# Layer 3 of a four-layer image kernel: a sum of squares on TensorE, two one-operand sums on ScalarE

## The chip, the cores and the metric

The kernel runs on one core of a Trainium2 chip. The metric is the device time of one execution in microseconds (us): the median of three runs is 34541.69 us, from 34539.79 to 34548.45.

## The reference, cut to what matters

Four layers follow one another on an image of 256x256 positions with 128 channels, all in fp32: an attention layer, a state-space layer, a Fourier layer, and a gated complex recurrence with 16 steps. Each adds to its input, after a group normalisation. Only the fourth (called layer 3) is touched. Its core, for every position and 64 complex channels, is:

```python
forget_gate = jax.nn.sigmoid(x_ri @ Wf + bf + 2.0)
input_gate = jax.nn.sigmoid(x_ri @ Wi + bi)
delta = jax.nn.softplus(x_ri @ Wd + bd) * 0.1
...
Ar, Ai = (A_ri[..., :c], A_ri[..., c:])
mag = jnp.sqrt(Ar ** 2 + Ai ** 2 + 1e-08)
scale = 0.95 * jax.nn.sigmoid(mag) / (mag + 1e-08)
Ar = Ar * scale
Ai = Ai * scale
...
def step(h_state, _):
    h_r, h_i = h_state
    Ah_r = Ar * h_r - Ai * h_i
    Ah_i = Ar * h_i + Ai * h_r
    return ((fg_r * Ah_r + inp_r, fg_i * Ah_i + inp_i), None)
```

A_ri and B_ri are the two-dimensional spectra of small 7x7 kernels. The kernel replaces the 16 steps by a closed form: the step is a 2x2 matrix, whose 16th power and the sum of whose powers follow from its determinant d and half trace t by repeated squaring.

## The kernel before, in words

The program runs one layer after the other. Layer 3 (layer3, L1358) works through 64 blocks of 1024 positions. A block is held as 8 tiles of 128 positions; `full` is [128, 8, 2, 64] (real and imaginary parts, 1024 elements in each partition) and `half` is [128, 8, 64] (512 elements). Five generators hold the work of a block:

- spectra(b) (L1416) loads x and the column spectra, evaluates the row spectra with eight matmuls (tile sps, L1428; two of them share one of two PSUM banks), copies them to sp by ScalarE (L1432), squares them (amp, L1435), adds the two squares (sq, L1437, VectorE), takes the magnitude as exp(0.5 ln) (mag, L1440 and L1441), adds 1e-8 (more, L1444, VectorE), and calls inverse (L1406): a first reciprocal by ln and exp on ScalarE (m_r, L1409 and L1410) and a correction of two VectorE operations (m_i, L1412 and L1413).
- gates(b) (L1448) takes the sigmoid of mag (sg, L1451), and for each of the 8 tiles makes two matmuls into one of three PSUM banks (gp, L1456 with the data, L1457 with the bias) and two ScalarE reads of it (fi, a sigmoid, L1458; dx, a copy, L1459).
- inputs(b) (L1463) makes the scale, the softplus (tail, L1474 to L1476, then L1489 and L1491), the squared size (sizes, L1479, which reads sq) and the input v.
- steps(b) (L1495) makes d (two products, L1507), t and their squares (L1511, ScalarE), x = 1 - t (L1541, VectorE), den (L1543), its inverse (d_r and d_i), and the two combinations that end in mv (L1567) and v (L1568).
- finish(b) (L1571) sums minus mv, minus v and the transposed x in PSUM (rp, L1579 to L1582), copies that out by ScalarE (o, L1585) and stores it.

The main loop (L1599) goes block by block. In its first half it alternates gates(b) with the first four parts of steps(b-1), and runs finish(b-2); in its second half it alternates the rest of steps(b-1), inputs(b) and spectra(b+1). ScalarE has two sets of tables to switch between in every block: one for ln and exp (loaded at L1606) and one for the sigmoid (loaded at L1451).

Two things set the order in which instructions stand in the queues. ScalarE keeps the order in which the program is written (L1595 asks for a written-out schedule of that engine alone). For the other engines a planner chooses the order when the program is built, from its own costs; the order is fixed from then on, and each engine takes its instructions in that order. From the third block on, every block has the same order on VectorE, and nearly every one on TensorE.

[...] Layer 3 uses seven: three for gp, two for sps, two for rp.

Of the kernel before, what the change touches and what calls it, by code (L numbers as in the profile page):

```python
# [10 lines left out]
F32 = mybir.dt.float32  # L11
AF = mybir.ActivationFunctionType
ALU = mybir.AluOpType
AX = mybir.AxisListType
PSUM = bass.MemoryType.PSUM
# [1342 lines left out]
def layer3(c, x3, out, ab):  # L1358
# [4 lines left out]
    tc, nc, t = c.tc, c.nc, c.t  # L1363
# [3 lines left out]
    full, half = [P, NT, 2, 64], [P, NT, 64]  # L1367
    with ExitStack() as a:
# [5 lines left out]
        wk = a.enter_context(tc.tile_pool(name="l3_wk", bufs=2))  # L1374
        tmp = a.enter_context(tc.tile_pool(name="l3_tmp", bufs=1))
        ps_g = a.enter_context(tc.tile_pool(name="l3_pg", bufs=3, space=PSUM))
        ps_s = a.enter_context(tc.tile_pool(name="l3_ps", bufs=2, space=PSUM))
        ps_r = a.enter_context(tc.tile_pool(name="l3_pr", bufs=2, space=PSUM))

        wall = one.tile([P, 4, P], F32, name="l3_wall")  # L1380

# [14 lines left out]
        tiny = one.tile([P, 1], F32, name="l3_tiny")  # L1396
# [3 lines left out]
        def swapped(m):  # L1400
            return m[:, :, ::-1]

        def twice(m):
            return m[:, :, None].to_broadcast(full)

        def inverse(x, scale, name):  # L1406

            first = tmp.tile(half, F32, name=f"{name}_r")
            nc.scalar.activation(first, x, AF.Ln, scale=scale)  # L1409
            nc.scalar.activation(first, first, AF.Exp, scale=-1.0)  # L1410
            inv = wk.tile(half, F32, name=f"{name}_i")
            nc.vector.scalar_tensor_tensor(inv, x, scale, first, ALU.mult, ALU.mult)  # L1412
            nc.vector.scalar_tensor_tensor(inv, inv, 2.0, first, ALU.subtract, ALU.mult)  # L1413
            return inv

        def spectra(b):  # L1416

            k = blocks[b] = {}
            k["x"] = io.tile([P, BL], F32, name="l3_x")
            nc.sync.dma_start(k["x"], x3[:, bass.ts(b, BL)])  # L1420
            tu = io.tile([14, 4, 256], F32, name="l3_tu", bufs=2)
            nc.sync.dma_start(tu, spec[bass.ts(b, 4)].rearrange("u r f -> r u f"))

            sp = k["sp"] = wk.tile([P, NT, 4, 64], F32, name="l3_sp")
            for i in range(NT):
                if i % 2 == 0:
                    sps = ps_s.tile([P, 2, 256], F32, name="l3_sps")
                nc.tensor.matmul(  # L1428
                    sps[:, i % 2], phase[:, bass.ts(i % 2, P)], tu[:, i // 2], start=True, stop=True
                )  # L1430
                if i % 2 == 1:
                    nc.scalar.copy(sp[:, i - 1 : i + 1].rearrange("p t k c -> p t (k c)"), sps)  # L1432
            yield
            amp = tmp.tile(full, F32, name="l3_amp")
            nc.scalar.activation(amp, sp[:, :, 0:2], AF.Square)  # L1435
            sq = k["sq"] = wk.tile(half, F32, name="l3_sq")
            nc.vector.tensor_tensor(sq, amp[:, :, 0], amp[:, :, 1], ALU.add)  # L1437
            yield
            mag = k["mag"] = wk.tile(half, F32, name="l3_mag")
            nc.scalar.activation(mag, sq, AF.Ln, bias=tiny)  # L1440
            nc.scalar.activation(mag, mag, AF.Exp, scale=0.5)  # L1441
            yield
            more = tmp.tile(half, F32, name="l3_more")
            nc.vector.tensor_scalar(more, mag, 1e-8, None, ALU.add)  # L1444
            k["inv"] = inverse(more, 1.0, "l3_m")
            yield

# [47 lines left out]
        def steps(b):  # L1495


            k = blocks[b]
            f, aa, v = k["fi"][:, :, 0:2], k["aa"], k["v"]
            have = {}  # L1500

            def new(name):
                return have.get(name) or tmp.tile(half, F32, name=f"l3_{name}")

            def mul(name, x, y):
                have[name] = new(name)
                nc.vector.tensor_tensor(have[name], x, y, ALU.mult)  # L1507

            def square(name, x):
                have[name] = new(name)  # L1510
                nc.scalar.activation(have[name], x, AF.Square)  # L1511

            def stt(name, x, s, y, op0, op1):
                have[name] = new(name)
                nc.vector.scalar_tensor_tensor(have[name], x, s, y, op0, op1)

            w = have

            mv = k["mv"] = wk.tile(full, F32, name="l3_mv")
            mu = tmp.tile(full, F32, name="l3_mu")  # L1520
            mul("d", f[:, :, 0], f[:, :, 1])
            mul("d", w["d"], k["size"])
            square("d2", w["d"])
            square("d4", w["d2"])
            have["f"] = new("f")
            nc.vector.tensor_tensor(w["f"], f[:, :, 0], f[:, :, 1], ALU.add)
            mul("t", aa[:, :, 0], w["f"])
            square("t2", w["t"])
            square("d8", w["d4"])
            yield  # L1530
            nc.vector.tensor_tensor(mv, v, twice(aa[:, :, 0]), ALU.mult)
            stt("t2", w["d"], -2.0, w["t2"], ALU.mult, ALU.add)
            square("t4", w["t2"])
            yield
            nc.vector.tensor_tensor(mu, swapped(v), twice(aa[:, :, 1]), ALU.mult)
            stt("t4", w["d2"], -2.0, w["t4"], ALU.mult, ALU.add)
            square("t8", w["t4"])
            yield
            stt("m", w["t"], 2.0, w["t2"], ALU.mult, ALU.mult)
            have["x"] = new("x")  # L1540
            nc.vector.tensor_scalar(w["x"], w["t"], -1.0, 1.0, ALU.mult, ALU.add)  # L1541
            have["den"] = new("den")
            nc.vector.tensor_tensor(w["den"], w["x"], w["d"], ALU.add)  # L1543
            stt("t8", w["d4"], -2.0, w["t8"], ALU.mult, ALU.add)
            square("tt8", w["t8"])
            yield
            mul("m", w["m"], w["t4"])
            w["inv"] = inverse(w["den"], 2.0, "l3_d")
            mul("m", w["m"], w["t8"])
            yield  # L1550
            stt("e", w["m"], 0.5, w["t"], ALU.mult, ALU.mult)
            stt("e", w["d8"], 2.0, w["e"], ALU.mult, ALU.add)
            have["ee"] = new("ee")
            nc.vector.tensor_tensor(w["ee"], w["e"], w["tt8"], ALU.subtract)
            nc.vector.tensor_tensor(mv[:, :, 0], mv[:, :, 0], mu[:, :, 0], ALU.subtract)
            yield
            stt("a", w["ee"], 2.0, w["m"], ALU.add, ALU.subtract)
            mul("md", w["m"], w["d"])
            stt("b", w["ee"], 2.0, w["x"], ALU.add, ALU.mult)
            nc.vector.tensor_tensor(mv[:, :, 1], mv[:, :, 1], mu[:, :, 1], ALU.add)  # L1560
            yield
            nc.vector.tensor_tensor(w["b"], w["b"], w["md"], ALU.add)
            nc.vector.tensor_tensor(mv, mv, f, ALU.mult)
            mul("a", w["a"], w["inv"])
            mul("b", w["b"], w["inv"])
            yield
            nc.vector.tensor_tensor(mv, mv, twice(w["a"]), ALU.mult)  # L1567
            nc.vector.tensor_tensor(v, v, twice(w["b"]), ALU.mult)  # L1568
            yield
# [25 lines left out]
        a.enter_context(tc.manual_schedule(engines={mybir.EngineType.Activation}))  # L1595
        tc.keep_in_program_order(nc.scalar.preload_act_table_set(EXP_LN))
        run(spectra(0))
        going = iter(())
        for b in range(NB + 2):  # L1599
            turns = gates(b) if b < NB else iter(())  # L1600
            for i in range(4):
                next(turns, None)
                next(going, None)
                if i == 1 and b >= 2:
                    run(finish(b - 2))
            tc.keep_in_program_order(nc.scalar.preload_act_table_set(EXP_LN))  # L1606
            run(
                going,
                *([inputs(b)] if b < NB else []),
                *([spectra(b + 1)] if b + 1 < NB else []),  # L1610
            )
            going = steps(b) if b < NB else iter(())
# [107 lines left out]
```

## Time and profile before

| | |
|---|---|
| median of three runs | 34541.69 us |
| the profiled execution, its own time | 34537.54 us |
| its span, first to last instruction | 34535.8 us |
| layer 3 with the preparation of its kernels' spectra | from about 32380 us to the end of the span, 2156 us |
| VectorE busy in these 2156 us | 2044.7 us |
| TensorE busy (matmul) in them | 1791.8 us |
| ScalarE busy in them | 1505.0 us |
| GpSimd busy in them | 0 us |
| mean granted TensorE clock in them | 0.81 |

The profile comes from one execution. PE is TensorE's matmuls and PEld its weight loads, DVE is VectorE, ACT is ScalarE, POOL is GpSimd; L1437 is line 1437 of the kernel. Tile names are cut, so that l_sq stands for l3_sq. One fp32 matmul leaves two records, and the ends of matmuls are modelled, so that starts are the better measure of their rate. An arrow (<-) behind a group or an instruction names what released it after an idle time; such releasers are inferred. A busy share is not a bound by itself: what counts is which wait ends last.

### The profile page before, as it was taken

The numbers are of one execution on the slowest core, as the hardware profiler recorded it, in microseconds if no ns is written. First come the engines' busy times: TensorE is split into PE (matmuls) and PEld (weight loads), VectorE is DVE, ScalarE is ACT, GpSimd is POOL, SyncE is SP. The second block draws the span as 40 slices with busy tenths as digits, with TensorE's granted clock in tenths as the row PEclk, the third lists the DMA queues.
The fourth block names the chain that finished last, engine by engine and source line by source line (L and its number), as shares of the span: only waits on it lengthen the run. The fifth ranks groups of instructions, "written<-read, shape, count | busy, mean of one in ns | idle before, by whom it ended". The sixth has DMA issues, their size and how long they took to land. (4 is left out here: it accounts for less than half of the span.)

```text
span 34535.8 us, 255681 instructions
## 1 busy us (share of the span) xinstructions
PE 29222.5 (85%) x72564; PEld 12231.8 (35%) x72564; DVE 31354.0 (91%) x24089; ACT 22500.8 (65%) x46445; POOL 26717.0 (77%) x6484
## 2 busy tenths in 40 slices
PE   7999888888888888888888888888888888899888
PEld 2554333333333333333333333333333333334444
DVE  5668899999999999999999999999999999863699
ACT  3665577777777777777777777777777777532476
POOL 2441199999999999999999999999999999620000
PEclk8999999999999999999999999999999999999888
DMA  3113655555555555555555555555555555674111
GB/s 136 45 45 99 155 190 190 191 191 191 189 191 191 190 190 192 191 190 191 195 201 200 202 201 199 202 204 200 201 202 200 201 202 202 213 236 147 66 34 33
DMA packets 2367335, 5947.80 MB, mean 172 GB/s; under 512 B 637447, under 2 KB 1639704, under 8 KB 1792086
## 3 DMA queue, kind: packets, MB, share of 16 engines
q1 hardware_dynamic: 2230742, 5864.31, 47.6%
q10 hardware_dynamic: 135168, 67.13, 0.6%
q8 instruction: 572, 9.37, 0.1%
q14 instruction: 853, 6.99, 0.1%
HBM read 5238.41 MB, written 692.58 MB: 172 GB/s over the span
## 5 line engine op out<-in xcount | busy, mean ns | idle before, releaser
L769 DVE TENSOR_TENSOR_SCAN l1b_h<-l1b_da,l1b_state,l1b_db 128x1024 f32<-128x1024 f32 x8192 | 18793.1, 2336 | 596.1 <-ACT l1b_db L758 583.8
L784 POOL TENSOR_TENSOR l1b_hc<-l1b_h,l1b_cc 128x2048 f32<-128x2048 f32 x4096 | 18446.0, 4528 | 329.2 <-DVE l1b_h L769 328.4
L803 PE MATMUL l1b_y<-l1b_hc,ident 128*128 128x512 f32 x32768 | 16052.8, 639 | 1117.9 <-POOL l1b_hc L784 1117.8
L754 ACT ACTIVATE l1b_da<-l1b_dl,l_A 128x512 f32<-128x512 f32 (+1 forms) x16384 | 11297.5, 690 | 3156.7 <-DVE l1b_h L769 2848.5
L803 PEld LDWEIGHTS l1b_y<-l1b_hc,ident 128*128 128x128 f32 x32768 | 6524.5, 205 | 10687.1 <-issue 8157.6
L736 POOL TENSOR_TENSOR l1b_db<-l1b_bb,l1b_dus 128x2048 f32<-128x2048 f32 x1536 | 6966.8, 4536 | 1245.2 <-DMA l1b_bb<-l1b_bc 1245.2
L736 DVE TENSOR_TENSOR l1b_db<-l1b_bb,l1b_du 128x2048 f32<-128x2048 f32 x2048 | 4658.4, 2275 | 35.2
L758 ACT ACTIVATE l1b_db<-l1b_state,l1b_db,l1b_af 128x1 f32<-128x1 f32 x8192 | 3045.1, 372 | 0.0
L675 PE MATMUL l1b_mm<-l1b_xd,l_dtw 41*128 41x512 f32 x2048 | 1374.6, 756 | 1714.1 <-ACT l1b_dus L725 1708.3
L701 PE MATMUL l1b_mm<-l1b_tail,ident 128*128 128x512 f32 x2048 | 1292.2, 717 | 1388.4 <-ACT l1b_tail L695 1388.4
L780 ACT COPY l1b_state<-l1b_h 128x4 f32<-128x4 f32 x4095 | 789.7, 193 | 2433.5 <-DVE l1b_h L769 2433.4
L326 POOL TENSOR_TENSOR l0b_e<-l0b_e,l0b_den 128x1024 f32<-128x1024 f32 x512 | 969.0, 1893 | 1403.0 <-DVE l0b_den L325 784.3
L701 PE MATMUL l1b_mm<-l1b_relu,ident 128*128 128x512 f32 x2048 | 1307.4, 727 | 0.0
L675 PEld LDWEIGHTS l1b_mm<-l1b_xd,l_dtw 41*128 41x128 f32 x2048 | 338.0, 206 | 2528.5 <-ACT l1b_dus L725 2131.4
L725 ACT COPY l1b_dus<-l1b_mm 128x512 f32<-128x512 f32 x512 | 299.6, 585 | 1388.2 <-DVE l1b_db L736 1387.7
L736 DVE TENSOR_TENSOR l1b_db<-l1b_bb,l1b_mm 128x2048 f32<-128x2048 f32 x512 | 1171.5, 2288 | 18.2 <-ACT l1b_dus L725 0.7
L302 DVE CUSTOM_DVE_ANT_0 l0b_e<-l0b_sc,l0b_bias 128x256 f32<-128x256 f32 x2048 | 745.5, 420 | 419.0 <-PE l0b_sc L291 415.7
L701 PEld LDWEIGHTS l1b_mm<-l1b_tail,ident 128*128 128x128 f32 x2048 | 377.1, 207 | 2059.0 <-ACT l1b_tail L695 1814.6
L493 DVE SCALAR_TENSOR_TENSOR l1a_mm<-l1a_xi,l1a_each,l1a_mm 128x512 f32<-128x512 f32 x1408 | 1046.1, 755 | 59.1 <-issue 13.0
L643 PE MATMUL l1b_du<-l1b_xc,l_xproj 128*40 128x512 f32 x2048 | 981.5, 602 | 62.4 <-DMA l_xproj<-in_l_xproj 58.8
L317 ACT ACTIVATE l0b_e<-l0b_e,l0b_top 128x256 f32<-128x256 f32 x2048 | 1012.2, 498 | 1.9 <-DVE l0b_top L302 1.9
L709 ACT COPY l1b_dl<-l1b_mm 128x512 f32<-128x512 f32 x1024 | 587.5, 574 | 524.5 <-DVE l1b_du L717 517.0
(256 smaller groups left out, 28744.8 us busy)
## 6 DMA issues: line engine op xcount, KB each, us to landing
l1b_bb<-l1b_bc SPq DMA_DIRECT2D x2048, 1024.0 KB
l1b_cc<-l1b_bc SPq DMA_DIRECT2D x2048, 1024.0 KB
l1b_xc<-l_xc SPq DMA_DIRECT2D x128, 1024.0 KB
l_y<-l1b_yo SPq DMA_DIRECT2D x128, 1024.0 KB
l1b_xc<-l_xct SPq DMA_DIRECT2D x128, 1024.0 KB
l_y<-l1b_yo SPq DMA_DIRECT2D x256, 512.0 KB
l_xc<-l1a_o SPq DMA_DIRECT2D x64, 1024.0 KB
l_xct<-l1a_ot SPq DMA_DIRECT2D x16, 4096.0 KB
```

Of the source, the lines that this page charges most:

```text
L317: nc.scalar.activation(e[:, i], e[:, i], AF.Exp, scale=-1.0, bias=top[:, i : i + 1], accum_out=den[:, i : i + 1],)
L326: nc.gpsimd.tensor_tensor(e, e, den[:, :, None].to_broadcast([P, 4, S]), ALU.mult)
L493: nc.vector.scalar_tensor_tensor(mm, xis[i][:, r + dy : r + dy + 2, dx : dx + S], each[:, dh, tap : tap + 1], mm, ALU.mult, ALU.add,)
L643: nc.tensor.matmul(du1[:40], w["xproj"][:, dh, k, :], blocks[ch][0][:, dh, cols(ch)], start=dh == 0, stop=dh == 1,)
L675: nc.tensor.matmul(mm, w["dt"][:, chunks[ch][0], dh * P : dh * P + P], xds[ch % 3][0:41], start=True, stop=True,)
L701: nc.tensor.matmul(mm, c.ident, part, start=i == 0, stop=i == 1)
L736: eng.tensor_tensor(db, bbs[g // 2], du[:, None, :].to_broadcast([P, G, CH]), ALU.mult)
L754: nc.scalar.activation(da[:, o + lo : o + hi], dl[:, lo:hi], AF.Exp, scale=w["A"][:, k, dh, n : n + 1])
L758: nc.scalar.activation(first, states[k][:, dh, two : two + 1], AF.Identity, scale=af[:, two : two + 1], bias=first,)
L769: nc.vector.tensor_tensor_scan(h_, a_, d_, states[k][:, dh, one : one + 1], ALU.mult, ALU.add)
L784: nc.gpsimd.tensor_tensor(hc, hs[g], ccs[g // 2], ALU.mult)
L803: nc.tensor.matmul(ys[j % 2], c.ident, hc[:, i], start=False, stop=j // 2 * G + i == 15)
```

## The change

Three operations leave VectorE. The sum of the two squares, sq, becomes two accumulating matmuls of the identity with the two halves of amp, into a PSUM bank that no other tile uses (a new pool with one buffer, the eighth bank); mag and sizes then read sq from PSUM. The addition of 1e-8, more, and the negation x = 1 - t become activations of ScalarE with the function Identity, with a pointer operand as the bias. Nothing else is edited. In the changed program lines after the new pool are moved down by one, those after the sum by two.

```diff
@@ -1376,6 +1376,7 @@
         ps_s = a.enter_context(tc.tile_pool(name="l3_ps", bufs=2, space=PSUM))
         ps_r = a.enter_context(tc.tile_pool(name="l3_pr", bufs=2, space=PSUM))
+        ps_q = a.enter_context(tc.tile_pool(name="l3_pq", bufs=1, space=PSUM))
@@ -1433,15 +1434,16 @@
             amp = tmp.tile(full, F32, name="l3_amp")
             nc.scalar.activation(amp, sp[:, :, 0:2], AF.Square)
-            sq = k["sq"] = wk.tile(half, F32, name="l3_sq")
-            nc.vector.tensor_tensor(sq, amp[:, :, 0], amp[:, :, 1], ALU.add)
+            sq = k["sq"] = ps_q.tile(half, F32, name="l3_sq")
+            for i in range(2):
+                nc.tensor.matmul(sq, c.ident, amp[:, :, i], start=i == 0, stop=i == 1)
             yield
             mag = k["mag"] = wk.tile(half, F32, name="l3_mag")
             nc.scalar.activation(mag, sq, AF.Ln, bias=tiny)
             nc.scalar.activation(mag, mag, AF.Exp, scale=0.5)
             yield
             more = tmp.tile(half, F32, name="l3_more")
-            nc.vector.tensor_scalar(more, mag, 1e-8, None, ALU.add)
+            nc.scalar.activation(more, mag, AF.Identity, bias=tiny)
             k["inv"] = inverse(more, 1.0, "l3_m")
@@ -1538,7 +1540,7 @@
             have["x"] = new("x")
-            nc.vector.tensor_scalar(w["x"], w["t"], -1.0, 1.0, ALU.mult, ALU.add)
+            nc.scalar.activation(w["x"], w["t"], AF.Identity, scale=-1.0, bias=c.ones[:, 0:1])
             have["den"] = new("den")
             nc.vector.tensor_tensor(w["den"], w["x"], w["d"], ALU.add)
```

## The prediction

> **What bounds the kernel now.** I went from the page's slices to the groups by line, the sums over stretches, the waits, and last the instructions of one block in order of time. The changed lines run only after 32380 us, in layer 3 (64 blocks); the first fence gives that stage and then three consecutive blocks, each from one load of the exp/log table (L1606) to the next. Columns: stretch, length, busy time (x instructions) of PE, PEld, DVE, ACT, POOL, granted clock, DMA share, GB/s.
>
> ```profile
> 32380.00:34536.00 2156.00, 1791.78 (x4608) 942.76 (x4608) 2044.69 (x2816) 1505.02 (x2754) 0.00 (x0) 0.81 0.11 33
> ...
> 32998.87:33032.47 33.60, 28.49 (x74) 15.17 (x73) 32.45 (x45) 23.43 (x43) 0.00 (x0) 0.80 0.11 34
> 33032.47:33066.07 33.60, 28.50 (x74) 14.95 (x73) 32.45 (x46) 23.52 (x44) 0.00 (x0) 0.80 0.11 33
> 33066.07:33097.97 31.90, 26.80 (x74) 14.24 (x73) 30.74 (x44) 23.43 (x44) 0.00 (x0) 0.84 0.12 35
> ```
>
> A block takes 33.03 us on average; VectorE (DVE) is busy but for 1.15 us. So layer 3 looks VectorE-bound, and the three removed operations are its own. But the block is also a ring through all engines. Two of the removed groups (count, busy us, mean ns, idle before), and the waits of the stage (who waited for whom: us in total, times, longest):
>
> ```profile
> L1541 DVE TENSOR_SCALAR l_x<-l_t 128x512 f32<-128x512 f32 x61 | 25.8, 423 | 0.0
> L1444 DVE TENSOR_SCALAR l_more<-l_mag 128x512 f32<-128x512 f32 x61 | 25.6, 420 | 0.0
> ```
> ```profile
> ACT l_d L1511 <- DVE l_d L1507: 194.3, 60, 3.2
> ...
> DVE l_sq L1437 <- ACT l_amp L1435: 67.4, 60, 1.3
> ACT l_mag L1440 <- DVE l_sq L1437: 46.8, 61, 1.3
> ```
>
> ScalarE (ACT) issues in written order. It has only 3.24 us of slack per block, at d (L1511). One block in order of time (start, length), ACT, then PE, then DVE:
>
> ```profile
> 33010.04 1.06 ACT L1435 ACTIVATE l_amp<-l_sp 128x1024 f32<-128x1024 f32 x1
> 33011.86 0.72 ACT L1440 ACTIVATE l_mag<-l_sq,l_tiny 128x512 f32<-128x512 f32 x1 [0.76 <-DVE l_sq L1437]
> 33012.61 0.63 ACT L1441 ACTIVATE l_mag<-l_mag 128x512 f32<-128x512 f32 x1
> 33013.93 0.63 ACT L1409 ACTIVATE l_m_r<-l_more 128x512 f32<-128x512 f32 x1 [0.69 <-DVE l_more L1444]
> 33014.60 0.63 ACT L1410 ACTIVATE l_m_r<-l_m_r 128x512 f32<-128x512 f32 x1
> ...
> 33021.48 1.29 ACT L1511 ACTIVATE l_d<-l_d 128x512 f32<-128x512 f32 x2 [3.24 <-DVE l_d L1507]
> ```
> ```profile
> 33005.63 7.17 PE L1428 MATMUL l_sps<-l_tu,l_phase 14*128 14x256 f32 x16 [2.83 <-ACT l_sp L1432]
> 33015.09 2.07 PE L1579 MATMUL l_rp<-l_mv,l_less 128*128 128x512 f32 x2 [2.29 <-DVE l_mv L1567]
> 33016.96 1.91 PE L1580 MATMUL l_rp<-l_v,l_less 128*128 128x512 f32 x2
> 33018.66 1.36 PE L1456 MATMUL l_gp<-l_wall,l_x 128*128 128x512 f32 x2
> ```
> ```profile
> 33016.08 0.69 DVE L1412 SCALAR_TENSOR_TENSOR l_m_i<-l_more,l_m_r 128x512 f32<-128x512 f32 x1
> ...
> 33020.76 0.69 DVE L1507 TENSOR_TENSOR l_d<-l_d,l_sizes 128x512 f32<-128x512 f32 x1
> ```
>
> Each fp32 matmul shows as two records. Where amp ends (33011.10), PE is still in 16 half-matmuls of sps; and it is at half clock: halves of 512 columns start 0.85 apart here (33016.96 to 33018.66 is two), 0.43 apart later. The clock records show it in every steady block: half rate for 10.2 or 13.7 us from about the start of sps, after PE has stood 2.8 us.
>
> [...] 0.85 against 0.43 us, half-rate stretches of 3 or 4 times 3.41. [...] here 0.72 us with tiny as bias (L1440) against 0.63 without (L1441).
>
> **The change part by part.** t counts from a block's table load (33000 block: 32998.87). In the changed program's instruction order the three operations are gone from DVE, ACT has more and x in their written places, and PE has the two sq matmuls after all 8 sps matmuls, ahead of rp, in every steady block.
>
> *DVE.* Starts are 0.60 apart for a two-operand 512, 0.34 for a tensor_scalar: 0.60+0.34+0.34 = 1.28 us less per block, and the 1.15 us wait for amp leaves DVE. Alone: 33.03-2.43 = 30.6 us.
>
> *sq on PE.* Four half-matmuls. Before PE reaches them, sps has to be issued: in the three blocks the last sps half is done being fed at t = 13.73, 13.20, 12.68, after amp's end (12.23 in the first). Cold, the fourth half starts 3 x 0.85 later and takes 1.06 to be readable (rp's cold record), 0.04 to be seen: ACT's mag starts at M = 13.73+3.65 = 17.38 (16.85, 16.33) instead of 12.99. If warm: 1.28+0.59+0.04 = 1.91, both ends kept. I take cold: it warmed only after a full window of 128-row matmuls; sps (14 rows) never did it, and sq is 3.4 us long, as a window is.
> The single bank costs nothing: the next sq waits for sizes (L1479) to have read the last one, and sizes starts at 33004.54, over 9 us before PE is through with sps; in the new order it stands as far ahead of mv as before. Reading sq from PSUM: nothing (L1437 was of the same width; PSUM reads elsewhere on the page, 2288 against 2275 ns at L736).
>
> *more on ACT.* It removes the 0.69 wait and adds one activation with pointer bias: 0.75+0.66+0.75+0.66+0.63 = 3.45 from M to the end of m_r, 3.37 now: +0.08, even.
>
> *What is late next.* DVE's m_i (L1412) waits for m_r, and behind it in DVE's queue stand tail, m_i, v, d, f and d (L1507), for which ACT's squares wait. From 33016.08 to 33021.45 that is 5.37, +0.04: ACT goes on at D = M+3.45+5.41 = M+8.86. Now D is M+9.62, since DVE comes late to m_i; from there the wait is ACT's doing.
>
> *From D to the next table load.* d2 to d8 and the fi/dx pair of tile 2: dx read by D+2.87. Three gate banks, so tile 5's matmuls may start there; tiles 5, 6, 7 at 1.72 each (four warm halves): D+8.08, readable D+8.28. Then fi, dx 0.54, the new x 0.67, tt8 0.65: D+10.14 (now 10.99, where PE came late). x stands on this path: +0.67 on ACT; its cover, DVE's 0.34, was free.
>
> Sum: M+19.0 = 36.4, 35.85, 35.3; mean 35.85, against 33.03: +2.8 us in a block. DVE then idles 5.2 us at m_i. About 62 steady blocks (64 less the first and the drain): 62 x 2.8 = 175 us. The profiled execution took 34537.5 (span 34535.8), 4.2 below the median of the runs; 175 on the median 34541.7 gives **34715 us**, +0.5%.
>
> **Bounds.** The half-clock edge sits on a free grid. If it falls late, only the last of the four sps tiles is cold, sps ends near 11.45 and M is 15.1: 34.1 us, +66 in all: 34608. If PE, now stopped up to 3 us for dx of tile 0, falls back to half rate in the gates too, tiles 5 to 7 come about 1.4 us later: 37.8, +296: 34838.
>
> **Rivals.**
> - *VectorE stays the bound: faster.* Place: the gap from amp's end to mag. If PE keeps full clock through sps and sq, sps ends near 10.45, sq follows amp, M is about 12.4, the ring is 31.4 us and the DVE floor 30.6: -1.6 x 62 = -100: 34442. It decides from M below 14.0 (M+19.0 below 33.03). For it: sq fills PE's 2.3 us of idleness. Against: the half clock in all steady blocks. 0.09.
> - *Late edge: no change.* The 34.1 us block, 34608, or a mixture of it with warmer blocks; "no change" is within 0.2% (69 us), about what a measurement can tell. Against: blocks before had the edge at t = 6.8 to 7.9, and PE's standstill starts no later. 0.09.
> - *Gates at half clock as well*: slower still, 34838; part of the forecast's side, 0.07.
> - My forecast: slower by the ring, 0.75.
>
> **Range.** 34580 to 34830: from a little under the late edge to the second bound; left out are the faster case, a few of the no-change ones and some 3 in 100 above. Slower by over 0.2%: 0.82; within: 0.09; faster: 0.09.
>
> **What would show it.** Block length 35 to 36.5; ACT's mag waiting 4 to 5 us on PE's sq; sq halves 0.85 apart; DVE's only long wait 5 us before m_i on ACT's m_r, its busy time about 30.5+0.7 a block; ACT still waiting 2.5 us before d. I am wrong if sq halves are 0.43 apart, if sq starts right after amp, or if DVE shows no wait at m_i.

## The result and the profile after

The changed kernel takes 34816.64 us (median of four runs, 34805.3 to 34818.93), against 34540.74 us (34534.36 to 34548.45) for four runs of the kernel before taken with it: a ratio of 1.0079, 95% interval 1.0066 to 1.0092, or +276 us. The forecast was 34715 us, so the sign was right, and of the loss only 175 us were foreseen. The profiled execution has a span of 34817.2 us.

All of it lies in layer 3, which is now 2437 us long from 32380 us to its end, against 2156: +281 in the two profiled executions. Then two consecutive blocks, each from one load of the exp/log table (now L1608) to the next. Columns as before: stretch, length, busy time and instructions of PE, PEld, DVE, ACT, POOL, granted clock, DMA share, GB/s.

```profile
32380.00:34817.00 2437.00, 2019.80 (x4872) 1044.98 (x4870) 1980.17 (x2634) 1585.80 (x2882) 0.00 (x0) 0.82 0.10 30
33009.67:33047.04 37.37, 31.57 (x77) 16.32 (x76) 30.91 (x42) 24.74 (x45) 0.00 (x0) 0.82 0.09 30
33047.04:33084.24 37.20, 31.56 (x77) 16.48 (x76) 30.92 (x42) 24.75 (x46) 0.00 (x0) 0.82 0.10 30
```

VectorE did get its relief: it works 30.9 us in a block instead of 32.45 in a 33.6 us block. Yet the block grew. VectorE is no longer the engine that is always busy, and the waits of the stage say why (who waited for whom: us in total, times, longest).

```profile
DVE l_m_i L1413 <- ACT l_m_r L1411: 350.1, 60, 6.1
ACT l_mag L1442 <- PE l_sq L1439: 319.8, 60, 5.5
...
PE l_gp L1458 <- ACT l_dx L1461: 144.6, 67, 2.5
ACT l_d L1513 <- DVE l_d L1509: 141.2, 59, 2.4
```

The two new waits are those of the forecast: ACT stands 5.3 us a block for sq, and DVE 5.8 us at m_i. Before, mag waited 0.8 us. Next comes the block that starts at 33009.67, in order of time (start, length): ACT, then PE, then DVE's one long wait.

```profile
33020.44 1.06 ACT L1436 ACTIVATE l_amp<-l_sp 128x1024 f32<-128x1024 f32 x1
33026.95 0.69 ACT L1442 ACTIVATE l_mag<-l_sq,l_tiny 128x512 f32<-128x512 f32 x1 [5.45 <-PE l_sq L1439]
...
33035.82 1.29 ACT L1513 ACTIVATE l_d<-l_d 128x512 f32<-128x512 f32 x2 [2.41 <-DVE l_d L1509]
...
33047.04 1.28 ACT L1608 ACT_TABLE_LOAD   x1
```
```profile
33016.43 6.77 PE L1429 MATMUL l_sps<-l_tu,l_phase 14*128 14x256 f32 x16 [3.45 <-ACT l_sp L1433]
33023.13 3.78 PE L1439 MATMUL l_sq<-l_amp,ident 128*128 128x512 f32 x4
33026.70 2.10 PE L1581 MATMUL l_rp<-l_mv,l_less 128*128 128x512 f32 x4
...
33032.91 1.12 PE L1458 MATMUL l_gp<-l_wall,l_x 128*128 128x512 f32 x2 [2.35 <-ACT l_dx L1461]
33033.87 1.81 PE L1459 MATMUL l_gp<-l_ball,ones 128*128 128x512 f32 x2
```
```profile
33030.41 0.69 DVE L1413 SCALAR_TENSOR_TENSOR l_m_i<-l_more,l_m_r 128x512 f32<-128x512 f32 x1 [5.73 <-ACT l_m_r L1411]
```

amp is read out at 33021.50, but PE, at half clock (0.51 granted, as the table below shows), is in sps until 33023.1, and the four halves of sq then take 3.78 us. One thing the forecast kept as a bound is visible too: PE stands 2.35 us for the dx of a gate tile, and from just after that the two bias halves (L1459) take 1.81 us instead of the 1.02 of the later tiles. The same block, cut close to where the granted clock changes, shows a second half-rate stretch, where the gates run:

```profile
33009.67:33016.76 7.09, 3.64 (x10) 1.44 (x9) 7.00 (x11) 6.98 (x9) 0.00 (x0) 1.00 0.00 1
33016.76:33026.98 10.22, 10.22 (x21) 6.28 (x20) 7.92 (x10) 2.37 (x5) 0.00 (x0) 0.51 0.02 6
33026.98:33033.81 6.83, 4.47 (x16) 2.36 (x16) 3.40 (x4) 6.27 (x11) 0.00 (x0) 0.99 0.00 0
33033.81:33037.22 3.41, 3.41 (x6) 1.29 (x5) 3.41 (x6) 1.37 (x3) 0.00 (x0) 0.52 0.00 0
33037.22:33047.04 9.82, 9.82 (x30) 4.95 (x29) 9.18 (x14) 7.76 (x20) 0.00 (x0) 0.99 0.33 107
```

Read the clock (third number from the end): 0.51 for 10.22 us, which is sps and sq, then 0.52 for one stretch of 3.41 us. The granted clock of layer 3 changes only on a grid of 3.413 us, before as after (10.24 us is three steps of it); one step is called a window here.

The chain of waits through the block (start, length, what; the piece of the chain from sq to the gates):

```profile
33023.20 3.73 PE l_sq L1439 x4
...
33026.95 0.70 ACT l_mag L1442
...
33031.69 0.63 ACT l_sg L1453
...
33032.59 0.27 ACT l_dx L1461
...
33032.91 1.12 PE l_gp L1458 x2
33034.03 1.65 PE l_gp L1459 x2
```

It runs from sq through ACT into PE's gates. It does not pass through DVE's m_i, where the forecast had put it.

### The profile page after: what moved, and what is told of

Same layout as the page of the kernel before. It is cut to its first block, busy times and chain, and to the rows that moved or that the text cites. A ratio compares the mean times of both kernels' runs of the same rounds, so it can differ in the third digit from the quotient of the medians.

```text
span 34817.2 us, 256069 instructions
## 1 busy us (share of the span) xinstructions
PE 29450.3 (85%) x72820; PEld 12331.7 (35%) x72820; DVE 31289.5 (90%) x23897; ACT 22592.5 (65%) x46573; POOL 26725.0 (77%) x6484
```

## The experiments: which part costs

The forecast's theory was: sq behind the cold sps (cold: at half clock, 0.51 above; warm: at full clock, 0.99 to 1.00) delays mag, and the delay goes on by m_i and d. The rivals were that the two sums on ScalarE, or the place of sq in the queue, carry the loss. "Before" below is always the kernel before on the same chip (medians 34538.96, 34545.94 and 34537.2 us in the three groups of runs). One thing bears on all of them: the planner's order of VectorE's and TensorE's instructions is not the same in these programs (it comes round every three blocks in the first run, every two in the second), so an edit can also change that order. ScalarE keeps the order that is written.

**Only sq on TensorE.** more and x stay on VectorE.

```diff
-            nc.scalar.activation(more, mag, AF.Identity, bias=tiny)
+            nc.vector.tensor_scalar(more, mag, 1e-8, None, ALU.add)
...
-            nc.scalar.activation(w["x"], w["t"], AF.Identity, scale=-1.0, bias=c.ones[:, 0:1])
+            nc.vector.tensor_scalar(w["x"], w["t"], -1.0, 1.0, ALU.mult, ALU.add)
```

> Only the sum of squares goes to TensorE; more and x stay on VectorE. Theory (the ring through sq: TensorE reaches it late and at half clock, so that ScalarE's mag, VectorE's m_i and d, and ScalarE's squares come late): nearly all of the change's +276 us is here. Per block 0.08 us less for more and up to 0.67 less for x than with the whole change, so 36.8 to 37.5 us a block instead of 33.08: +230 to +270 us. Rival (the two additions to ScalarE's queue): under +100 us.

Measured: 34740.59 us, ratio 1.0058 (1.0043 to 1.0073), +202. sq alone is slower by most of the loss; the size expected of it was missed. But this program is not the changed kernel less the two sums. Its order on VectorE and TensorE comes round every three blocks, where the kernel before and the changed kernel have one order for their steady blocks. A long block and the short one behind it, VectorE, then TensorE, then the stretch at half rate:

```profile
33072.28 0.43 DVE L1446 TENSOR_SCALAR l_more<-l_mag 128x512 f32<-128x512 f32 x1 [4.39 <-ACT l_mag L1443]
33072.62 1.22 DVE L1569 TENSOR_TENSOR l_mv<-l_mv,l_a 128x1024 f32<-128x1024 f32 x1
...
33103.51 1.21 DVE L1569 TENSOR_TENSOR l_mv<-l_mv,l_a 128x1024 f32<-128x1024 f32 x1
...
33109.82 0.43 DVE L1446 TENSOR_SCALAR l_more<-l_mag 128x512 f32<-128x512 f32 x1 [3.96 <-ACT l_mag L1443]
```
```profile
33073.90 2.07 PE L1581 MATMUL l_rp<-l_mv,l_less 128*128 128x512 f32 x2 [3.03 <-DVE l_mv L1569]
...
33108.19 2.44 PE L1581 MATMUL l_rp<-l_mv,l_less 128*128 128x512 f32 x4
```
```profile
33061.52:33078.59 17.07, 14.04 (x24) 7.11 (x23) 12.68 (x16) 7.79 (x13) 0.00 (x0) 0.50 0.01 3
33099.07:33109.31 10.24, 10.24 (x20) 5.97 (x19) 6.79 (x9) 3.07 (x5) 0.00 (x0) 0.50 0.02 6
```

In two blocks of three, mv stands behind more in VectorE's queue, and more waits for mag, which waits for sq. So TensorE stands 3.03 us for mv, and the half rate goes on for 17.07 us, into the gates: the block takes 37.54 us here. In the third, mv stands ahead of more, TensorE goes on to rp at once, the half rate ends after 10.24 us, and the block takes 34.16 us. The 202 us are thus the cost of sq in this order, in part by a wait that the changed kernel does not have; they are not a share of the 276.

**Only the two sums on ScalarE.** sq stays on VectorE.

> Only more and x go to ScalarE; the sum of squares stays on VectorE. Theory: more takes 0.75 us where ScalarE waited 0.69, x costs up to 0.67 on ScalarE between the last gate and the next table load, VectorE gains 0.68: between -30 and +45 us. Rival (the two additions to ScalarE's queue make the loss): +150 us or more. The planner orders VectorE somewhat differently here, which neither theory counts.

Measured: 34533.42 us, ratio 0.9998 (0.999 to 1.0007): -5.5 us, no change. The two sums alone are free, in the order that the planner made for this program; it comes round every two blocks, and the steady blocks take 31.5 to 34.1 us. The two halves of the change add up to +197, together they cost +276 (the intervals of the first part and of the whole just overlap). As each half has an order of its own, no run shows what the 79 us between the two figures come from.

**Half of sq.** Only the real part's square is summed; the imaginary square is left out.

```diff
-            for i in range(2):
-                nc.tensor.matmul(sq, c.ident, amp[:, :, i], start=i == 0, stop=i == 1)
+            nc.tensor.matmul(sq, c.ident, amp[:, :, 0], start=True, stop=True)
```

> The changed kernel with only the first of sq's two matmuls, so the imaginary part's square is left out. Theory (after sq two chains of equal length close the ring, through m_i and d and through the first gate read and TensorE's gates, so what is saved before mag is saved in the block): mag starts 1.7 us earlier, a block takes about 35.7 us, unless the grid of the clock holds it; +120 to +220 us over before. Rival (the wait in the queue and the crossing between engines cost it, the matmul's length is hidden): +255 to +285 us, as the changed kernel.

Measured: 34640.18 us, ratio 1.0028 (1.0017 to 1.0039), +94, below what either side expected. Taking away 1.7 us of sq gives back 182 us, more than 1.7 x 62 = 105, which is the most that the length of the wait explains. The rest fits the clock. Of 59 steady blocks 7 have the second half-rate stretch, at the gates, where the changed kernel has it in 52; the blocks take 33.6 to 36.2 us.

**sq first.** Half of the sixteen sps halves that stand ahead of sq on PE already belong to the block after. One order edge holds the first of these behind sq; further edges keep VectorE's order as in the changed kernel, and the rest of TensorE's order stays too.

```diff
+                if i == 0 and qs[0]:
+                    behind(s_, qs[0])
...
+                qs[0] = nc.tensor.matmul(sq, c.ident, amp[:, :, i], start=i == 0, stop=i == 1)
```

> The changed kernel, with one edge of order more: the next block's first sps matmul stands behind sq in TensorE's queue, so that sq follows its own block's sps and starts when amp is there. The order of VectorE is as in the changed kernel. Theory: mag starts about 1.4 us earlier (15.8 instead of 17.3 after the table load), since sq no longer waits for eight half-matmuls of sps, while TensorE comes to its gates later by as much; a block takes 36 to 37.4 us: +180 to +265 us over before. Rival (the place in the queue is the main cost): a block of 33 us, +60 us or less.

Measured: 34694.72 us, ratio 1.0046 (1.0031 to 1.0061), +157, between what the two sides expected. mag's wait shrinks from 5.45 to 3.87 us; sq now starts as soon as amp is there, after PE stood 1.76 us for it, but still takes 3.78 us:

```profile
33304.10 3.78 PE L1449 MATMUL l_sq<-l_amp,ident 128*128 128x512 f32 x4 [1.76 <-ACT l_amp L1446]
```

The place in the queue is worth some 118 us of the 276, and is not the main cost. Part of the 118 is the clock's: the gates have a half-rate stretch in 22 of 59 steady blocks here, instead of 52.

## The experiments: the path, and the clock

**m_i out of the way.** If the delay goes on by m_i, moving it behind d should win time. The two corrections are issued with the next block's inputs.

```diff
-            inv = wk.tile(half, F32, name=f"{name}_i")
-            nc.vector.scalar_tensor_tensor(inv, x, scale, first, ALU.mult, ALU.mult)
-            nc.vector.scalar_tensor_tensor(inv, inv, 2.0, first, ALU.subtract, ALU.mult)
-            return inv
+            def rest():
+                inv = wk.tile(half, F32, name=f"{name}_i")
+                nc.vector.scalar_tensor_tensor(inv, x, scale, first, ALU.mult, ALU.mult)
+                nc.vector.scalar_tensor_tensor(inv, inv, 2.0, first, ALU.subtract, ALU.mult)
+                return inv
+            return rest
...
+            k["inv"] = k["inv"]()
```

> The changed kernel with the two corrections m_i issued with the next block's inputs, so that on VectorE d no longer stands behind m_i and its wait for m_r. sq stays on TensorE. Theory (behind m_i waits the whole of d, and with it ScalarE): ScalarE goes on to d about 2.4 us earlier, TensorE's gates then bound the second half; a block takes about 35.6 us instead of 37.55: +120 to +190 us over before. Rival (VectorE's wait at m_i is off the path, and only shows the slack it has): unchanged, +260 to +290 us.

Measured: 34814.02 us, ratio 1.008 (1.0063 to 1.0097), +275: nothing won. That the delay goes on by m_i and d, and by them alone, is refuted. ACT in one block of it:

```profile
33014.85 0.69 ACT L1445 ACTIVATE l_mag<-l_sq,l_tiny 128x512 f32<-128x512 f32 x1 [5.45 <-PE l_sq L1442]
...
33021.15 1.32 ACT L1517 ACTIVATE l_d<-l_d 128x512 f32<-128x512 f32 x2
...
33035.36 1.28 ACT L1612 ACT_TABLE_LOAD   x1
```

ACT's d no longer waits: it comes at M+6.30 instead of M+8.87. But the next table load stays at M+20.51 (M+20.09 in the block of the changed kernel). The time goes to the gates, whose matmuls start when the dx of a tile is read, whatever m_i does. After that wait TensorE is slow here too, as the bias halves behind it (L1462) take 1.82 us, those of the later tiles 1.02:

```profile
33020.79 1.12 PE L1461 MATMUL l_gp<-l_wall,l_x 128*128 128x512 f32 x2 [2.80 <-ACT l_dx L1464]
```

So mag has two paths behind it: by m_i and d on DVE, and by the sigmoid's table load, dx and the gates on PE. The first alone would end at M+19.0 by the forecast's working, the second ends at M+20.09 in the changed kernel, as its gates are cold for a stretch (0.52 for 3.41 us). The second is the later one, and shortening the first wins nothing. Even in blocks whose gates stay at full clock little is won: the load comes at M+18.83 here (14 of 59 steady blocks) and at M+19.04 in the changed kernel (7 of 59). The test is not quite pure, since the planner also placed some other VectorE operations and one gate tile differently.

**Four filling matmuls ahead of sps.** They multiply the identity by a resident tile, 512 columns each, into sq's own bank, before sps, to keep PE busy where it stood. Nothing reads them. Order edges keep DVE's order and that of sq before rp.

```diff
+            sq = k["sq"] = ps_q.tile(half, F32, name="l3_sq")
+            for i in range(4):
+                nc.tensor.matmul(sq, c.ident, wall, start=True, stop=True)
```

> The changed kernel with four matmuls more per block (identity by the gate weights, 512 columns) into sq's bank, ahead of sps, where TensorE stood 3.5 us; sq overwrites them. The order of VectorE's instructions is held as in the changed kernel. Theory (half clock after the standstill doubles sps and sq): sps, sq and the gates run at full clock, mag starts near 12.4 us after the table load instead of 17.3, a block takes 31 to 32 us: 65 to 130 us faster than before. Rival (it is the place in the queue and the crossing between engines, not the clock): a block stays above 36 us, +180 us or more, since TensorE only got more to do.

Measured: 34606.86 us, ratio 1.002 (1.0012 to 1.0028), +68. 208 of the 276 us come back, though sq stays where it was; neither theory had that number. Now sps runs at full clock, and the clock falls only for sq:

```profile
33025.10:33028.99 3.89, 3.89 (x18) 2.86 (x17) 3.89 (x6) 2.23 (x3) 0.00 (x0) 0.98 0.05 15
33028.99:33032.40 3.41, 3.41 (x5) 1.43 (x6) 3.41 (x4) 0.00 (x0) 0.00 (x0) 0.52 0.00 0
33032.40:33051.58 19.18, 16.29 (x50) 8.00 (x49) 15.68 (x23) 15.28 (x33) 0.00 (x0) 1.00 0.18 56
```

The odd thing: PE was busy all through the stretch ahead of the fall, 3.89 of 3.89 us. What it did there were sps matmuls, and these fill 14 of 128 rows.

**Zero rows for sps.** The operands of sps are padded from 14 to 128 rows with zeros, set once; the sum is the same. First together with the four filling matmuls:

```diff
+        phase = one.tile([P, 256], F32, name="l3_phase")
+        nc.vector.memset(phase, 0.0)
+        nc.sync.dma_start(phase[0:14], t["c_phase_w"])
...
+            tu = tus[b % 2]
+            nc.sync.dma_start(tu[0:14], spec[bass.ts(b, 4)].rearrange("u r f -> r u f"))
```

> The kernel of e5 (changed, with four matmuls more before sps), and the sps operands padded with zero rows from 14 to 128. In e5 the clock fell to half at the end of sps, in spite of two fully busy windows, and sq ran at half clock. Theory (matmuls of 14 rows do not count as activity for the clock): with 128 rows the clock holds, sq's halves are 0.43 us apart, mag starts 13.4 us after the table load, a block takes 31.5 to 33 us: 0 to 90 us faster than before. Rival (rows do not matter, the fall has another cause): as e5, +50 to +85 us.

Measured: 34492.35 us, ratio 0.9985 (0.9978 to 0.9992), -54 us. The clock is at 1.00 from one end of a 200 us stretch to the other:

```profile
33000.00:33200.00 200.00, 178.94 (x526) 88.73 (x525) 188.51 (x252) 153.58 (x280) 0.00 (x0) 1.00 0.11 34
```
```profile
33026.89 3.70 PE L1445 MATMUL l_sps<-l_tu,l_phase 128*128 128x256 f32 x16
33030.54 1.99 PE L1454 MATMUL l_sq<-l_amp,ident 128*128 128x512 f32 x4
```

With 14 rows sps took 3.79 us at full clock and sq 3.66 after it; with 128 rows sps takes 3.70 and sq 1.99. Here the whole change, at full clock, beats the kernel before. This run and the one with the filling matmuls alone have the same instructions in the same order on all three engines, in a steady block; they differ in the rows.

**Zero rows alone.** The changed kernel with the padding and no filling matmuls; in a steady block every engine has the same instructions in the same order as in the changed kernel.

> The changed kernel with the sps operands padded with zero rows from 14 to 128, no filling matmuls; the same order of instructions on all engines. Theory (the standstill of 3.5 us before sps drops the clock, and sps of 14 rows keeps it down): the clock still drops, but a full window of sps brings it back before sq is through, so sq runs half or wholly at full clock and the gates are not hit: a block of 33 to 35.5 us, 0 to +150 us. Rival (only the filling matmuls helped): as the changed kernel, +255 us or more.

Measured: 34593.08 us, ratio 1.0016 (1.001 to 1.0023), +56. So 220 of 276 us go away without one instruction more or less in a block, by more rows alone. After the standstill of 3.44 us before sps the granted clock is still low, 0.56 over the first 3.50 us of sps, but it is 1.00 over the 9.74 us behind these, and sq runs at full rate, 1.98 us:

```profile
33319.70 5.30 PE L1434 MATMUL l_sps<-l_tu,l_phase 128*128 128x256 f32 x16 [3.44 <-ACT l_sp L1438]
33324.96 1.98 PE L1444 MATMUL l_sq<-l_amp,ident 128*128 128x512 f32 x4
...
33332.94 2.03 PE L1463 MATMUL l_gp<-l_wall,l_x 128*128 128x512 f32 x2 [2.34 <-ACT l_dx L1466]
```

The second fall, at the gates, remains: behind the 2.34 us standstill the clock is 0.53 over 3.66 us. The block is locked at 34.13 us. M, the start of mag after the table load, is 14.04, and 14.04 + 20.09 = 34.13: everything behind mag is as late as in the changed kernel, and only M has moved.

**The kernel before, with filling matmuls.** Four into the free bank, written ahead of sps; no other edit. It asks what the clock is worth there.

> The kernel before with four matmuls more per block into the free bank (identity by the last two dx tiles, results not used), where TensorE stood before sps. Theory (the half clock after the standstill is a cost of the kernel before too): sps and rp run faster, a block takes about 32 us instead of 33.06, VectorE's own 31.8 being the floor: 30 to 80 us faster. Rival (before, VectorE bounds and the clock is covered): within 15 us.

Measured: 34508.4 us, ratio 0.9989 (0.9983 to 0.9996), -37.5 us. The half rate falls from 12.55 to 8.50 us a steady block (the granted clock is 0.86 from 33200 to 33400 us, against 0.81 in layer 3 before). That the clock alone wins the 37.5 us is not shown: the planner put gate matmuls between the filling ones and sps, and made an order that comes round every two blocks, of about 31.1 and 33.75 us.

**Two versions meant to win.** Both have three filling matmuls and padded rows, x on VectorE, and no operation for more: 1e-8 goes into the bias of the logarithm and into the first correction (add, then multiply). The first keeps sq on VectorE, the second has it on TensorE.

```diff
-            k["inv"] = inverse(more, 1.0, "l3_m")
+            k["inv"] = inverse(mag, 1.0, "l3_m", 1e-8)
...
+                nc.scalar.activation(first, x, AF.Ln, bias=tiny)
...
+                nc.vector.scalar_tensor_tensor(inv, x, more, first, ALU.add, ALU.mult)
```

> A version to beat both: the sum of squares and x on VectorE as before; more is dropped (its 1e-8 goes into the bias of the ln and into the first operation of the correction); three filling matmuls before sps and the zero rows as in e10. Theory: TensorE's clock holds, VectorE bounds with 31.5 us less what is hidden: a block of 31.3 to 32.3 us, 45 to 110 us faster than before. Rival (the half clock is not what keeps the kernel before at 33.06): within 25 us of before.

Measured: 34438.93 us, ratio 0.9969 (0.9957 to 0.998), -107.

> A second version to beat both: sq on TensorE with three filling matmuls and padded rows, more dropped as in e8 (its 1e-8 in the bias of the ln and in the correction), x back on VectorE. Theory: with the clock held the block is mag's start plus 19.04 us as in e10 (13.24 + 19.04 = 32.28), less 0.75 for more and up to 0.67 for x: 30.9 to 31.6 us, VectorE's floor being 30.9: 85 to 130 us faster than before. Rival (TensorE's gates or VectorE's order hold the block near e10's): 35 to 75 us faster.

Measured: 34415.67 us, ratio 0.9964 (0.995 to 0.9978), -121.5 us: faster than the kernel before and the changed one. Here VectorE is the bound at last, busy 397.45 of 400 us, with PE at full clock:

```profile
33000.00:33400.00 400.00, 358.35 (x1045) 176.77 (x1043) 397.45 (x538) 299.42 (x554) 0.00 (x0) 1.00 0.12 36
```

Against their own runs of the kernel before, the second gains 14.5 us more than the first, but the intervals overlap, so whether the move of sq itself wins here is not settled. At full clock it costs nothing that these runs can tell; the first version, though, still has half-rate stretches (4.22 us a block, and a granted clock of 0.93 from 33200 to 33400 us; none in the second, at 1.00).

## Why the prediction was right in its sign and too small in its size

The result lies in the range that was given, but by what the forecast had set down as its second bound, at 0.07, and not by its main case: blocks of 35 to 36.5 us were forecast, and steady blocks average 37.4. Point by point, by its own steps:

- *DVE*: right. With three operations gone DVE works 30.9 us in a block (about 31.2 forecast), and as the forecast said, the freed time became a wait at m_i: 5.8 us, against 5.2.
- *sq on PE*: the mechanism was right. sq stood behind sps, beginning at 33023.13 as sps ended, though amp was there at 33021.50; it was cold (0.51), and mag waited 5.45 us; the zero rows alone, which let sq run at full clock and change nothing else in a block, take 220 us of the loss away. The forecast for the first of its three blocks was M = 17.38; measured 17.28 in the block shown. But it took the mean of the three, 16.85. Over 59 steady blocks, from each table load to mag, M averages 17.44, as most blocks repeat at 17.45: +0.59 us a block. The blocks of before drifted against the clock's windows: their half rate begins 6.64 to 8.35 us after the load. Those of after are locked to them, 37.55 us being 11 windows of 3.413: from 33157 us on it begins 6.86 to 6.90 us after the load.
- *The single bank* and *more on ACT*: right. No wait at the bank shows. From M to the end of m_r it is 3.43 us (33026.95 to 33030.38), 3.45 forecast; more takes 0.72 us (L1446) and x 0.73 (L1543), with a pointer operand each; the exp of mag (L1443), of the same size and without one, takes 0.63.
- *What is late next*: its number is right, D = M+8.87 against M+8.86, and its meaning wrong. The step has m_i and d as the path that sets the end. They are one of two. The chain of waits of after goes over the other, by the gates on PE, and moving m_i changed nothing. In blocks with warm gates the end still came out at M+19.04, against M+19.0; as the two ways end some 0.2 us apart there, that was in part luck.
- *From D to the next table load*: this term was mis-sized, 10.14 forecast, 11.22 measured in the block shown and 11.11 on average. The working let PE take the gates warm. PE stood 2.35 us before a gate tile, and ran at half rate for one window from just after (0.52 over 3.41 us). In the 7 steady blocks without that stretch the term is 10.18, as forecast; in the other 52 it is 11.23. The forecast names exactly that as its second bound ("gates at half clock as well", 37.8 us, reckoned on its longest block, with 1.4 us for the stretch; it cost 1.05).

The two misses make the sum: 0.59 + 0.97 = 1.56 us a block, x 62 = 97, and 276 - 175 = 101. In absolute terms, 37.4 us a block (17.44 + 8.87 + 11.11) against 33.03 is 4.38 x 62 = 272.

The rival *VectorE stays the bound* was right in its condition, M below 14.0. With sps and sq at full clock (1.00) M is 13.24 (33019.33 to 33032.57), D to the load is back at 10.17, and the kernel is faster than before, by 54 us, as the first of the runs with zero rows showed. 100 were said, with M at 12.4; of the 0.8 us between, the filling matmuls account for nearly all, since sps starts 7.56 us after the load there, and 6.76 in the kernels without them. In the changed kernel the condition is not met.

What stays open is what sq and the two sums cost apart from each other, in one and the same order of instructions.

## What to carry to other kernels

Before an operation is moved to TensorE, look at what stands ahead of it in that queue and at the clock it will run at there: a fp32 sum of 512 columns that cost VectorE 0.60 us cost 3.78 us here, as its four halves ran at half rate (0.51) behind matmuls of 14 rows. When a delay has two ways round a ring, follow both to the end before moving one, and check each idle gap that the delay opens on TensorE for the half-rate stretch that may follow it (3.41 us of it behind a gap of 2.35 here). Before a part of a change is read as a share of the whole, compare the order of the instructions: the planner may have made another one. A forecast that treats the clock as an average should also price the case where blocks lock to its windows (11 of them, 37.55 us, here).

## What the runs showed of the hardware that was not expected

- Matmuls of 14 rows did not keep the clock up. The forecast had seen that sps, with 14 rows, never brought the full clock back: in its block, sps fills PE from 33005.69 to 33012.52, the clock is 0.50 there, and it is 0.50 until 33019.34. The runs show that sps also loses it. With filling matmuls ahead, PE was busy without a gap through 3.8 us of 14-row matmuls, and the clock fell at the end of that, to 0.52; with the same matmuls padded to 128 rows of zeros it held at 1.00. So in these runs the rows of the matmuls counted, and rows of zeros counted too. Row counts between 14 and 128 were not tried.
- The clock also fell, to 0.52 for one window, after a standstill of only 2.35 us, less than a window's 3.41. One figure tells the windows of the changed kernel apart. Laid on the grid on which the half-rate stretches begin and end, it has, between 32500 and 34734 us, 111 windows at full rate that half rate followed, and in each PE was busy, sps left out, for at most 1.40 us; in the 307 that full rate followed it was busy for at least 1.46. One window of each kind, with the one after it (busy PE stands behind the length, the clock third from the end):

```profile
33068.10:33071.51 3.41, 1.40 (x4) 0.68 (x5) 3.41 (x5) 2.50 (x6) 0.00 (x0) 1.00 0.00 0
33071.51:33074.92 3.41, 3.41 (x9) 1.86 (x8) 3.41 (x6) 1.87 (x4) 0.00 (x0) 0.50 0.00 0
...
32696.05:32699.46 3.41, 1.46 (x4) 0.74 (x5) 3.41 (x5) 2.44 (x6) 0.00 (x0) 1.00 0.00 0
32699.46:32702.87 3.41, 3.41 (x16) 1.97 (x14) 3.41 (x6) 1.93 (x4) 0.00 (x0) 1.00 0.09 10
```

  Their standstills are 2.19 and 2.15 us. The kernel before has, between 32500 and 34450 us, 58 windows at full rate that half rate followed, with at most 0.71 us of such work, and 295 that full rate followed, with at least 2.42. With sps counted, the 58 have up to 1.59 us, more than the 1.46 that was enough above. So in these two traces what tells the windows apart is how much of one of them PE spends on matmuls other than sps. The ends of matmuls are modelled, and so no sharper limit can be read off.
- The periodic blocks locked to these windows. The changed kernel repeats at 37.55 us (11 windows), and the runs that took away one cold stretch (the filling matmuls, the zero rows alone) at 34.13 us (10 windows). What was saved there shows as one whole window, 3.42 us a block.
